# Four of eight router weights spread by DMA and multiplied on GpSimd, and the depthwise taps summed in PSUM, in the last stage of a two-layer MetaFormer kernel

## The chip, the cores and the metric

The kernel runs on one core of one Trainium2 chip. The metric is the device time of one execution in microseconds. A core has five engines that work side by side, each through its own instructions in a fixed order: TensorE (PE in the profile; PEld is its weight load), VectorE (DVE), ScalarE (ACT), GpSimd (POOL) and SyncE (SP), which here issues the DMAs. They wait for each other through semaphores. SBUF and PSUM are the two on-chip memories, both with 128 partitions; products of TensorE land in PSUM, which has eight banks of 128x512 f32.

## The reference

Eight images of 128 channels and 64 x 64 pixels pass through two layers, each a token mixer and a mixture of experts. The change lies in the end of the second layer alone:

```python
    # end of the second mixer (L1_conv)
    out = _ln(out, norm2_w, norm2_b)
    out = out.transpose(0, 2, 1).reshape(B, C, H, W) + seed
    h1 = einsum('bchw,oc->bohw', out, fc1_w) + fc1_b            # 256 hidden channels
    dw = conv_general_dilated(h1, dw_w, (1, 1), 'SAME',
                              feature_group_count=256)           # depthwise, 3 x 3
    h2 = gelu(dw + dw_b)
    ffn = einsum('bohw,co->bchw', h2, fc2_w) + fc2_b
    return out + ffn                                             # added to x outside

    # second mixture of experts (L1_ffn), on layer-normed tokens, 8 experts, top 2
    router_probs = softmax(x @ router_w + router_b)
    top_p, top_i = top_k(router_probs, 2)
    top_p = top_p / sum(top_p)
    expert_out = einsum('bnd,edc->bnec', x, expert_w) + expert_b
    gathered = take_along_axis(expert_out, top_i[..., None], axis=2)
    return einsum('bnk,bnkc->bnc', top_p, gathered)
```

## The kernel before

The layers run one after the other. A selective scan in four directions over eight images takes the first half of the time, then come the first experts, and the second mixer's state-space layers. The last stage, `second_ffn`, is where the change lies. It works on 64 slices: eight images of eight slices, each of 128 channels by 512 pixels, which are eight image rows. All data are f32.

The stage is a software pipeline written as a list of steps. At time t of the loop, the step with offset `at` works on slice t - at, with the late steps first:

```python
            steps = [(0, load), (1, center), (2, scale), (3, hidden), (5, taps), (6, feed), (7, center2), (8, scale2),
                     (9, logits), (9 + RS, weights), (10 + RS, experts)]
```

with RS = 4. A scheduler then gives each engine its fixed order, from dependences, priorities, free buffers and its own costs; a tile pool's `bufs` says how many slices may hold a tile at once. So an instruction may stand some way from where the list has it. The steps are:

- `load`: three DMAs on SyncE's queue (ys, seed and x2; x2 shows as x in the profile).
- `center`, `scale`: layer norm. Two products with a matrix of 1/128 make mean and variance (ln_m, ln_v), VectorE subtracts (xc), ScalarE squares and does the reciprocal root as Ln and Exp (sq), GpSimd multiplies (ys) and adds to seed.
- `hidden`: the two halves of fc1 (h_p in the profile), written by ScalarE with the bias into h1 (h), a padded image of 66 x 66 for each half. Two images are kept.
- `taps`: per half, nine VectorE instructions with a per-partition weight. The first multiplies and adds the bias (L336), eight multiply and add (L339) into dw, an SBUF tile with four buffers. h1 is read at nine shifted places; a slice needs a row of the slices above and below it, which lie in the same padded image.
- `feed`: ScalarE's Gelu in place on dw, two products into f_p, the residual on VectorE and GpSimd (res).
- `center2`, `scale2`: the second layer norm, ending with GpSimd's multiply into yn.
- `logits`: per slice four small products into lg_p; after each fourth slice the router's top 2 for all four, some twenty small VectorE instructions (`route`).
- `weights`: transposes the slice's router weights to 8 rows (pt_p) and ScalarE copies them into pT, a tile of 128 rows that are zero from row 8 on.
- `experts`: a product with expert_b into o_p. Then for each of eight experts: a product of a selection matrix sel8 with pT spreads the expert's weights over 128 partitions (pb_p, L288), VectorE multiplies yn by it (xw, L330), and a product with the expert's matrix adds to o_p. A last VectorE add goes into res, and a DMA stores it (L1636).

Helpers hold the lines that the profile names: L288 is every matmul of `mm`, L330 `tt`, L336 and L339 `ts` and `stt`, L291 `act`. ScalarE swaps its function table around Gelu (two loads per slice). PSUM's eight banks go to the tags n (3 buffers: ln_m, ln_v, h1_p), f (1), lg (1), o (1) and pb (2).

Of the kernel before, what the change touches and what calls it, by code (L numbers as in the profile page):

```python
# [9 lines left out]
F32 = mybir.dt.float32  # L10
# [11 lines left out]
C = 128  # L22
# [256 lines left out]
class Net:  # L279
# [907 lines left out]
    def second_setup(self, pool, ps):  # L1187
# [3 lines left out]
        nc.vector.tensor_copy(self.sel8, bc(self.k("ident")[:, :8], 128))  # L1191
        self.pT = [pool.tile([128, S], F32, name=f"pT{q}") for q in range(2)]
        for t in self.pT:
# [266 lines left out]
    def second_ffn(self):  # L1460


        nc, tc = self.nc, self.tc
        pool = nc.gpsimd
        RS = 4
        NQ = RS * S // 128
# [3 lines left out]
        with tc.tile_pool(name="ff", bufs=1) as pl, tc.tile_pool(name="ffw", bufs=2) as wk, \  # L1470
                tc.tile_pool(name="ffps", bufs=1, space=PSUM) as ps:

            h1 = [[pl.tile([128, 66, 66], F32, name=f"h1_{q}{h}") for h in range(2)] for q in range(2)]
            for t in (*h1[0], *h1[1]):
                nc.vector.memset(t[:, 0:66:65, :], 0.0)
                nc.vector.memset(t[:, 1:65, 0:66:65], 0.0)
            gm = pl.tile([C, self.nb], F32, name="gm")
            nc.vector.tensor_reduce(gm, self.gms, AX.X, ALU.add)
            self.ts(gm, gm, 1.0 / L, ALU.mult)
            p = ps.tile([C, S], F32, tag="n", bufs=3, name="gm_p")  # L1480
            self.mm(p[:, : self.nb], self.mix.rearrange("p q c -> p (q c)"), gm)
# [19 lines left out]
            def squares(v, x):  # L1501

                p = bank("n", 3, "ln_m")
                self.mm(p, self.k("mean"), x)
                v["xc"] = tile_("xc", 4)
                self.tt(v["xc"], x, p, ALU.subtract)
                v["sq"] = tile_("sq", 4)
                self.act(v["sq"], v["xc"], AF.Square)

            def scaled(v, out):  # L1510
                p = bank("n", 3, "ln_v")
                self.mm(p, self.k("mean"), v["sq"])
                self.rsqrt(v["sq"], p, self.k("e5"))
                self.tt(out, v["xc"], v["sq"], ALU.mult, pool)
# [13 lines left out]
            def hidden(n):  # L1528
                v = made[n]
                b, s, sg = place(n)  # L1530
                for h in range(2):
                    p = bank("n", 3, "h1_p")
                    self.mm(p, self.w("fc1_w")[:, h * 128 : (h + 1) * 128], v["seed"])
                    self.act(h1[b % 2][h][:, 1 + 8 * s : 9 + 8 * s, 1:65], p.rearrange("p (r q) -> p r q", q=64),
                             AF.Identity, bias=self.w(f"fc1_b{h}"))

            def taps(n):
                v = made[n]
                b, s, sg = place(n)
                gelus = v["a"] = []  # L1540
                for h in range(2):
                    a = wk.tile([128, 8, 64], F32, name="dw", bufs=4)
                    for k in range(9):
                        x = h1[b % 2][h][:, 8 * s + k // 3 : 8 * s + k // 3 + 8, k % 3 : k % 3 + 64]
                        w = self.w(f"dw_w{h}")[:, k : k + 1]
                        if k == 0:
                            self.ts(a, x, w, ALU.mult, self.w(f"dw_b{h}"), ALU.add)
                        else:
                            self.stt(a, x, w, a, ALU.mult, ALU.add)
                    gelus.append(a)  # L1550

            def feed(n):
                v = made[n]
                self.silus_done([self.act(a, a, AF.Gelu_apprx_tanh) for a in v["a"]])
                f = bank("f", 1, "f_p")
                for h, a in enumerate(v.pop("a")):
                    self.mm(f, self.w(f"fc2_w{h}"), a.rearrange("p r q -> p (r q)"), start=h == 0, stop=h == 1)
                x = v["res"] = tile_("res", RS + 5)
                self.stt(x, f, self.w("fc2_b"), v["seed"], ALU.add, ALU.add)
                self.tt(x, x, v["x2"], ALU.add, pool)  # L1560
# [4 lines left out]
            def scale2(n):  # L1565
                v = made[n]
                v["yn"] = tile_("yn", RS + 4)
                scaled(v, v["yn"])
# [44 lines left out]
            def weights(n):  # L1613
# [3 lines left out]
                for c in range(S // 128):  # L1617
                    nc.tensor.transpose(p[:8, c * 128 : (c + 1) * 128], routed["now"][:, n % RS * (S // 128) + c, :],
                                        self.k("ident"))
                nc.scalar.copy(self.pT[n % 2][:8], p[:8])  # L1620

            def experts(n):
                v = made[n]
                b, s, sg = place(n)
                pT = self.pT[n % 2]
# [88 lines left out]
```

## Time and profile before

| | |
|---|---|
| runs, median (lowest to highest) of 3 | 21109.04 us (21099.6 to 21120.56) |
| profiled execution | 21100.1 us |
| its span | 21098.0 us |
| PE busy | 16896.5 us, 80% |
| DVE busy | 15973.0 us, 76% |
| ACT busy | 11555.9 us, 55% |
| POOL busy | 8894.3 us, 42% |
| `second_ffn`: first load issued, end of the span | 19303.83, 21098.0 us |

Shares are of the whole span, and most of it belongs to other stages; `second_ffn` is the last three and a half of the page's 40 slices of the span. The page's groups are by line, so one line of a helper holds operations from all stages, and tiles tell them apart. In a row of the groups the numbers behind the bar are the idle time of the engine just before these instructions and what ended it. Tile names lose their buffer numbers: h is h1, sel is sel8, m is a PSUM tile of the first scan.

### The profile page before, as it was taken

The numbers are of one execution on the slowest core, as the hardware profiler recorded it, in microseconds if no ns is written. First come the engines' busy times: TensorE is split into PE (matmuls) and PEld (weight loads), VectorE is DVE, ScalarE is ACT, GpSimd is POOL, SyncE is SP. The second block draws the span as 40 slices with busy tenths as digits, with TensorE's granted clock in tenths as the row PEclk, the third lists the DMA queues.
The fourth block names the chain that finished last, engine by engine and source line by source line (L and its number), as shares of the span: only waits on it lengthen the run. The fifth ranks groups of instructions, "written<-read, shape, count | busy, mean of one in ns | idle before, by whom it ended". The sixth has DMA issues, their size and how long they took to land. (4 is left out here: it accounts for less than half of the span.)

```text
span 21098.0 us, 301814 instructions
## 1 busy us (share of the span) xinstructions
PE 16896.5 (80%) x112733; PEld 8742.5 (41%) x112733; DVE 15973.0 (76%) x21079; ACT 11555.9 (55%) x17646; POOL 8894.3 (42%) x6004
## 2 busy tenths in 40 slices
PE   6777777777777777777887888888888888887999
PEld 2222222222222222222645666666666666664343
DVE  7979799797988979798354666666666666667886
ACT  6555555555555555555253555555555555555442
POOL 6757577575767757576011111212111121212221
PEclk9989899999999999899687999999999999998999
DMA  4434344343444434344441000000000000001110
GB/s 113 130 105 130 101 132 129 104 129 105 130 110 123 129 104 130 103 132 118 137 130 37 25 27 26 25 27 25 27 26 25 26 25 27 25 27 36 40 42 24
DMA packets 804471, 1616.93 MB, mean 77 GB/s; under 512 B 179579, under 2 KB 411931, under 8 KB 802267
## 3 DMA queue, kind: packets, MB, share of 16 engines
q1 hardware_dynamic: 803006, 1597.61, 27.6%
q8 instruction: 893, 14.63, 0.3%
q14 instruction: 572, 4.69, 0.1%
HBM read 1373.56 MB, written 223.74 MB: 76 GB/s over the span
## 5 line engine op out<-in xcount | busy, mean ns | idle before, releaser
L288 PE MATMUL dA<-parts,expand 128*128 128x512 bf16 x12288 | 3445.5, 390 | 2448.5 <-ACT dA L291 1770.3
L330 POOL TENSOR_TENSOR bx<-xE,B 128x1024 f32<-128x1024 f32 x2048 | 4823.0, 2358 | 703.7 <-DVE dA L622 461.9
L291 ACT ACTIVATE dA<-dA,negA 128x512 f32<-128x512 f32 x4096 | 2709.4, 661 | 3726.2 <-PE dA L288 3703.4
L622 DVE TENSOR_TENSOR_SCAN dA<-dA,last,bx 128x1024 f32<-128x1024 f32 x1536 | 3612.6, 2352 | 175.7 <-ACT dA L291 158.5
L288 PEld LDWEIGHTS <-expand 128*128 128x128 bf16 x12288 | 1195.4, 98 | 5231.3 <-issue 4517.6
L291 ACT ACTIVATE E_cm<-ss_p 128x1024 f32<-128x1024 f32 x2048 | 1976.9, 1030 | 1544.2 <-PE ss_p L288 1542.7
L339 DVE SCALAR_TENSOR_TENSOR E_cm<-E_cm,gm_cm 128x1024 f32<-128x1024 f32 x2048 | 2423.9, 1224 | 512.6 <-ACT E_cm L291 511.9
L330 DVE TENSOR_TENSOR hc<-dA,C 128x1024 f32<-128x1024 f32 x2048 | 2508.6, 1225 | 166.7 <-DVE dA L622 3.2
L1131 POOL COPY Sd_cm<-S_cm 64x128 f32<-64x128 f32 x1024 | 800.0, 781 | 2887.0 <-DVE S_cm L330 2754.0
L330 POOL TENSOR_TENSOR xD_cm<-tok_cm,D_cm 128x256 f32<-128x256 f32 x512 | 413.1, 807 | 2915.0 <-PE y_p L288 2795.1
L288 PE MATMUL y_p<-E_cm,pad_cm 128*32 128x128 f32 x32768 | 1389.7, 286 | 18.3 <-DVE E_cm L339 10.1
L288 PE MATMUL ss_p<-ssB_cm,ssA_cm 128*128 128x512 bf16 x4096 | 1242.6, 420 | 188.4 <-ACT E_cm L291 166.9
L622 DVE TENSOR_TENSOR_SCAN dA<-dA,bx 128x1024 f32<-128x1024 f32 x512 | 1174.1, 2293 | 185.4 <-POOL bx L330 130.2
L288 PE MATMUL y<-hc,kt 128*32 128x512 f32 x8192 | 1199.8, 653 | 26.0 <-DVE hc L330 26.0
L288 PEld LDWEIGHTS y_p<-E_cm,pad_cm 128*32 128x32 f32 x32768 | 940.5, 113 | 388.5 <-issue 240.6
L288 PE MATMUL bc_p<-stk_cm,W_cm 128*128 128x256 f32 x4096 | 1019.2, 392 | 23.8 <-DMA stk_cm<-xs 20.8
L330 DVE TENSOR_TENSOR gm_cm<-g_p,kt 128x1024 f32<-128x1024 f32 x512 | 624.3, 1219 | 505.8 <-PE g_p L288 501.0
L339 DVE SCALAR_TENSOR_TENSOR dw<-h,w_second,dw 128x512 f32<-128x512 f32 x1024 | 854.4, 860 | 5.1 <-ACT h L291 1.0
L291 ACT ACTIVATE tok_cm<-tok_p 128x384 f32<-128x384 f32 x1024 | 503.0, 491 | 605.6 <-PE tok_p L288 450.5
L288 PEld LDWEIGHTS bc_p<-stk_cm,W_cm 128*128 128x128 f32 x4096 | 739.9, 190 | 194.7 <-issue 76.8
L291 ACT ACTIVATE BC_cm<-bc_p 128x1024 f32<-128x1024 f32 x512 | 525.0, 1026 | 536.8 <-PE bc_p L288 532.4
L288 PE MATMUL tok_p<-W_cm,stk_cm 128*128 128x200 f32 x4096 | 761.4, 339 | 0.0
(387 smaller groups left out, 30190.7 us busy)
## 6 DMA issues: line engine op xcount, KB each, us to landing
xE<-dtx_d SPq DMA_DIRECT2D x2048, 512.0 KB
dtx_d<-dtx SPq DMA_DIRECT2D x256, 256.0 KB
x<-x SPq DMA_DIRECT2D x192, 256.0 KB
ssA_cm<-cs_cm SPq DMA_DIRECT2D x3072, 4.0 KB
stk_cm<-xs SPq DMA_DIRECT2D x368, 128.0 KB
stk_cm<-y SPq DMA_DIRECT2D x368, 128.0 KB
x<-in_x_dram SPq DMA_DIRECT2D x64, 256.0 KB
x<-r SPq DMA_DIRECT2D x64, 256.0 KB
```

The lines of the kernel that those rows point to most:

```text
L288: self.ordered(self.nc.tensor.matmul(out, lhsT=lhsT, rhs=rhs, start=start, stop=stop))
L291: i = self.ordered(self.nc.scalar.activation(out, in_, func, **kw))
L330: self.ordered((eng or self.nc.vector).tensor_tensor(out, a, b, op))
L339: self.ordered(self.nc.vector.scalar_tensor_tensor(out=out, in0=a, scalar=s, in1=b, op0=op0, op1=op1))
L622: self.ordered(nc.vector.tensor_tensor_scan(out=t, data0=t, data1=bx.pop(n), initial=0.0 if ch["j"] == 0 else last[:, q : q + 1], op0=ALU. ...
L1131: nc.gpsimd.tensor_copy(Sd[gr, :, g * hi : (g + 1) * hi], S2[gr])
```

## The change

Two edits go together in `second_ffn`.

The router weights of experts 4 to 7 take another way. `weights` writes their four rows of pT to DRAM by a DMA, and a second DMA reads them back to all 128 partitions (pb, 128x2048). A new step `weighted` multiplies yn by them on GpSimd (xwd, 128x512 each). `experts` spreads by a product and multiplies on VectorE for experts 0 to 3 alone; the two kinds alternate in the sum into o_p.

The taps sum into a PSUM tile dw with two buffers instead of SBUF with four; Gelu reads it and writes an SBUF tile. The banks come from n (3 to 2 buffers) and pb (2 to 1). h1 is kept per slice, ten rows of 66, in a ring of four: ScalarE writes a slice's eight rows and also, in instructions of their own, its first and last row into the neighbouring slices' tiles; GpSimd fills the border rows of an image's first and last slice.

`weights` moves one step later, `weighted` two steps behind it, and `experts` three steps later than it was. pT gets four buffers, res and yn three more.

```diff
-        self.pT = [pool.tile([128, S], F32, name=f"pT{q}") for q in range(2)]
+        self.pT = [pool.tile([128, S], F32, name=f"pT{q}") for q in range(4)]
...
+        NP = 4
...
-            h1 = [[pl.tile([128, 66, 66], F32, name=f"h1_{q}{h}") for h in range(2)] for q in range(2)]
-            for t in (*h1[0], *h1[1]):
-                nc.vector.memset(t[:, 0:66:65, :], 0.0)
-                nc.vector.memset(t[:, 1:65, 0:66:65], 0.0)
+            h1 = [[pl.tile([128, 10, 66], F32, name=f"h1_{q}{h}") for h in range(2)] for q in range(4)]
+            for q in h1:
+                for t in q:
+                    nc.vector.memset(t[:, :, 0:66:65], 0.0)
...
-                p = bank("n", 3, "ln_m")
+                p = bank("n", 2, "ln_m")
...
-                p = bank("n", 3, "ln_v")
+                p = bank("n", 2, "ln_v")
...
-                    p = bank("n", 3, "h1_p")
+                    p = bank("n", 2, "h1_p")
                     self.mm(p, self.w("fc1_w")[:, h * 128 : (h + 1) * 128], v["seed"])
-                    self.act(h1[b % 2][h][:, 1 + 8 * s : 9 + 8 * s, 1:65], p.rearrange("p (r q) -> p r q", q=64),
-                             AF.Identity, bias=self.w(f"fc1_b{h}"))
+                    p = p.rearrange("p (r q) -> p r q", q=64)
+                    own = h1[n % 4][h]
+                    if s == 0:
+                        pool.memset(own[:, :1], 0.0)
+                    if s == NS - 1:
+                        pool.memset(own[:, 9:], 0.0)
+                    for to, of in ((own[:, 1:9], p), *([(h1[(n - 1) % 4][h][:, 9:], p[:, :1])] * (s > 0)),
+                                   *([(h1[(n + 1) % 4][h][:, :1], p[:, 7:])] * (s < NS - 1))):
+                        self.act(to[:, :, 1:65], of, AF.Identity, bias=self.w(f"fc1_b{h}"))
...
-                    a = wk.tile([128, 8, 64], F32, name="dw", bufs=4)
+                    a = ps.tile([128, 8, 64], F32, tag="dw", bufs=2, name="dw")
                     for k in range(9):
-                        x = h1[b % 2][h][:, 8 * s + k // 3 : 8 * s + k // 3 + 8, k % 3 : k % 3 + 64]
+                        x = h1[n % 4][h][:, k // 3 : k // 3 + 8, k % 3 : k % 3 + 64]
...
-                self.silus_done([self.act(a, a, AF.Gelu_apprx_tanh) for a in v["a"]])
+                hs = [tile_("gelu", 4) for _ in v["a"]]
+                self.silus_done([self.act(h, a.rearrange("p r q -> p (r q)"), AF.Gelu_apprx_tanh)
+                                 for h, a in zip(hs, v.pop("a"))])
...
-                x = v["res"] = tile_("res", RS + 5)
+                x = v["res"] = tile_("res", RS + 8)
...
-                v["yn"] = tile_("yn", RS + 4)
+                v["yn"] = tile_("yn", RS + 7)
...
-                nc.scalar.copy(self.pT[n % 2][:8], p[:8])
+                pT = self.pT[n % len(self.pT)]
+                nc.scalar.copy(pT[:8], p[:8])
+                d = self.dp.tile([NP, S], F32, name="p_d", bufs=3)
+                nc.sync.dma_start(d, pT[8 - NP : 8])
+                made[n]["pb"] = wk.tile([128, NP, S], F32, name="pb", bufs=2)
+                nc.sync.dma_start(made[n]["pb"], bc(d, 128, 0))
+
+            def weighted(n):
+                v = made[n]
+                v["xw"] = []
+                for e in range(NP):
+                    xw = tile_("xwd", 2 * NP)
+                    self.tt(xw, v["yn"], v["pb"][:, e], ALU.mult, pool)
+                    v["xw"].append(xw)
...
                 for g in range(8):
-                    pb = bank("pb", 2, "pb_p")
-                    self.mm(pb, self.sel8[:, g, :], pT)
-                    xw = tile_("xw", 3)
-                    self.tt(xw, v["yn"], pb, ALU.mult)
-                    self.mm(o, self.w("expert_w")[:, g * 128 : (g + 1) * 128], xw, start=False, stop=g == 7)
+                    e = g // 2 + g % 2 * NP
+                    if e < 8 - NP:
+                        pb = bank("pb", 1, "pb_p")
+                        self.mm(pb, self.sel8[:, e, :], pT)
+                        xw = tile_("xw", 3)
+                        self.tt(xw, v["yn"], pb, ALU.mult)
+                    else:
+                        xw = v["xw"][e - 8 + NP]
+                    self.mm(o, self.w("expert_w")[:, e * 128 : (e + 1) * 128], xw, start=False, stop=g == 7)
...
             steps = [(0, load), (1, center), (2, scale), (3, hidden), (5, taps), (6, feed), (7, center2), (8, scale2),
-                     (9, logits), (9 + RS, weights), (10 + RS, experts)]
+                     (9, logits), (10 + RS, weights), (12 + RS, weighted), (13 + RS, experts)]
```

More of the change, by code (lines that the diff above doesn't have):

```diff
@@ L1479, in second_ffn @@
             self.ts(gm, gm, 1.0 / L, ALU.mult)
-            p = ps.tile([C, S], F32, tag="n", bufs=3, name="gm_p")
+            p = ps.tile([C, S], F32, tag="n", bufs=2, name="gm_p")
             self.mm(p[:, : self.nb], self.mix.rearrange("p q c -> p (q c)"), gm)
@@ L1553, in feed @@
                 v = made[n]
-                self.silus_done([self.act(a, a, AF.Gelu_apprx_tanh) for a in v["a"]])
+                hs = [tile_("gelu", 4) for _ in v["a"]]
+                self.silus_done([self.act(h, a.rearrange("p r q -> p (r q)"), AF.Gelu_apprx_tanh)
+                                 for h, a in zip(hs, v.pop("a"))])
                 f = bank("f", 1, "f_p")
-                for h, a in enumerate(v.pop("a")):
-                    self.mm(f, self.w(f"fc2_w{h}"), a.rearrange("p r q -> p (r q)"), start=h == 0, stop=h == 1)
-                x = v["res"] = tile_("res", RS + 5)
+                for h, a in enumerate(hs):
+                    self.mm(f, self.w(f"fc2_w{h}"), a, start=h == 0, stop=h == 1)
+                x = v["res"] = tile_("res", RS + 8)
                 self.stt(x, f, self.w("fc2_b"), v["seed"], ALU.add, ALU.add)
@@ L1624, in experts @@
                 b, s, sg = place(n)
-                pT = self.pT[n % 2]
+                pT = self.pT[n % len(self.pT)]
                 o = bank("o", 1, "o_p")
```

## The prediction

> **What bounds the kernel now.** The page's span is 21098.0 us and the profiled run took 21100.1, 9 below the median of the runs (21109.04). Everything is summed against 21100.1 and the 9 is added back. Up to the second FFN both programs hold the same instructions in the same order on every engine (two more small fills aside), so I read only the last 1.8 ms. First, busy time by stage: before the first expert (the loop fills), with everything running, and after the last tap (it drains).
>
> ```profile
> core 0: us, PE busy (x) PEld busy (x) DVE busy (x) ACT busy (x) POOL busy (x), PEclk, DMA share, GB/s
> 19285.00:19490.00 205.00, 128.98 (x331) 52.52 (x321) 155.30 (x220) 103.60 (x145) 68.53 (x38) 0.72 0.18 55
> 19490.00:20920.00 1430.00, 1323.51 (x3379) 569.11 (x3378) 1245.29 (x1938) 584.48 (x828) 350.01 (x218) 0.98 0.12 38
> 20920.00:21098.00 178.00, 164.29 (x395) 64.45 (x393) 66.24 (x110) 12.11 (x19) 5.03 (x4) 0.96 0.04 15
> ```
>
> Together 1813 us. TensorE is 93% and VectorE 87% busy in the middle; GpSimd 24%. The timeline of SyncE's queue gives the pace: the ys load before a pair of stores recurs every fourth slice.
>
> ```profile
> 20208.20 0.32 SPq L1499 DMA_DIRECT2D ys<-ys  x1
> ...
> 20310.54 0.32 SPq L1499 DMA_DIRECT2D ys<-ys  x1
> ```
>
> 102.34 us for four slices: 25.6 each. Next, the groups by line, 19600 to 20800 (46.9 slices), and the same operations elsewhere in the trace by tile or line (minimum/median/maximum ns).
>
> ```profile
> L339 DVE SCALAR_TENSOR_TENSOR dw<-h,w_second,dw 128x512 f32<-128x512 f32 x736 | 611.6, 851 | 3.8
> L330 DVE TENSOR_TENSOR xw<-yn,pb_p 128x512 f32<-128x512 f32 x365 | 242.3, 678 | 40.7 <-PE pb_p L288 40.0
> L330 POOL TENSOR_TENSOR ys<-xc,sq 128x512 f32<-128x512 f32 x47 | 85.5, 1819 | 93.7 <-issue 84.4 <-ACT sq L291 9.3
> L336 DVE TENSOR_SCALAR dw<-h,w_second 128x512 f32<-128x512 f32 x92 | 64.9, 707 | 45.3 <-PE f_p L288 45.3
> ```
>
> ```profile
> L339 DVE SCALAR_TENSOR_TENSOR dw<-h,w_second,dw x1024: 730/742/1799, 19322.9 to 20919.4; 128x512 f32<-128x512 f32 x171
> L339 DVE SCALAR_TENSOR_TENSOR m<-sp_u,m x256: 683/696/697, 111.3 to 9882.4; 128x512 f32<-128x512 f32 x128
> ```
>
> ```profile
> L330 DVE TENSOR_TENSOR hc<-dA,C x430: 1223/1225/1226, 4001.1 to 5996.5; 128x1024 f32<-128x1024 f32 x144
> ```
>
> The tap sum dw reads two SBUF tensors: usually 742 ns, but up to 1799, mean 851, and the long ones stand beside GpSimd multiplies, themselves stretched to a mean of 1819. In the scan stage GpSimd is 78% busy (4150 to 4250), yet m<-sp_u,m (one operand and the result in PSUM, the form that dw gets) never passes 697 and hc, with one PSUM operand, never 1226. So GpSimd and VectorE disturb each other where VectorE reads two SBUF tensors, and not where one of them is in PSUM.
>
> By start-to-start times in the timeline, a tap costs VectorE 0.66 us, a first tap 0.46, xw or xc 0.60, res 0.66 and 0.60, the router's small ones 1.6 per slice. Per slice: 16 x 0.66 + 2 x 0.46 + 8 x 0.60 + 2 x 0.60 + 1.26 + 1.6 = 20.3; the stretch adds 16 x 0.109 + 2 x 0.165 = 2.1 (851 and 707 against 742 and 542): 22.4. TensorE issues a 128x512 f32 matmul every 0.43 us, two per product: 50 x 0.43 + 1.3 (logits, transposes) = 22.8. Neither alone makes 25.6; they wait for each other for about 2.8.
>
> **Part by part.** *Four experts lose their spreading matmul and VectorE multiply.* TensorE: 8 x 0.43 = 3.4 less, 19.4 per slice. VectorE: 4 x 0.60 = 2.4 less.
>
> *Tap sums in PSUM.* The stretch goes: 2.1 less. The row m<-sp_u,m has the price, 696; dw also takes a per-partition scalar, so I keep 742 and 0.66. A VectorE instruction that follows directly on one whose PSUM result it reads starts later than one that doesn't: m to dt 0.73, dt to the scan 0.60.
>
> ```profile
> 3008.86 0.69 DVE L330 TENSOR_TENSOR m<-sp_u,m 128x512 f32<-128x512 f32 x1
> 3009.59 0.69 DVE L330 TENSOR_TENSOR dt<-sp_r,m 128x512 f32<-128x512 f32 x1
> 3010.19 2.35 DVE L622 TENSOR_TENSOR_SCAN dA<-dA,last,bx 128x1024 f32<-128x1024 f32 x1
> ```
>
> In the changed order (as the changed program's instructions stand on each engine) the two halves' chains alternate with other work: 10 of 1152 tap instructions follow directly on their own chain, so nothing here; at 0.13 for each of 18 it would be 2.3. The first tap lies between 0.46 and 0.60 (a multiply of the xw form): I add 0.1 in all. VectorE: 20.3 - 2.4 + 0.1 = 18.0.
>
> [...]
>
> *Two PSUM buffers for dw instead of four in SBUF.* The first tap of slice n+1 now waits on ScalarE's Gelu of n for the same half (before: on f_p, 45.3 us in 46.9 slices). After the last tap VectorE still has xc and the other half's first tap to do (0.60 + 0.46); Gelu needs about 0.69 (PSUM source, as sq<-ln_v) when ScalarE stands ready: hidden, or 0.5. If ScalarE is late by a table load (1.28), sq (0.62) and an h write (0.69), some 2.6.
>
> *One pb bank and two n banks instead of two and three.* In the changed order each pb product is followed by one or two other products before the two o products: 0.86 to 1.72 against 0.25 + 0.69 for the multiply. Covered mostly; 0 to 1 us.
>
> *GpSimd's four multiplies.* 4 x 1.27 (undisturbed 128x512, as yt<-yt,zs) = 5.1 to 4 x 1.8 = 7.3; with its own four, 10 to 14 us of a slice. They stand ahead of ys, seed, res and yn on GpSimd, and TensorE's h product waits for seed already (36.0 us, 13 times); but those four lose their stretch (means 1.39 to 1.82 now), so I take 0 net, up to 1.3.
>
> *Spread by DMA.* SyncE gets two issues per slice. The write waits for ScalarE's copy, the spread for the write (2.3 us, as dtx_d issue to xE issue) and for GpSimd's release two slices back; queued behind are stores and the loads of ys, seed and x2, which the order places three or more slices ahead of use. The stages leave two slices of cover; without it a round trip is 2.3 + 4.0 (the longest wait of bx for xE) = 6.3. 1 MB more per slice against a DMA share of 0.12: no collision.
>
> *Edge rows.* 3.5 ScalarE writes of 128x64 per slice at 0.22 (wd<-dec_p): 0.8 on an engine at 41% (584 of 1430). The border fills (32 small ones on GpSimd) and the further buffers of pT, res and yn: nothing that a slice would show.
>
> **The sum.** TensorE 19.4 and VectorE 18.0 bound the slice; waits stay about as before (2.8, less for fewer hand-overs, more for the bank waits): 22.0. The changed order holds 11.8 slices of taps before the first expert (before 9.0), 52.2 in the middle, 11.5 of experts behind the last tap (9.5). Fill: 168/9 = 18.7 per slice; there the stretch is larger (taps 923 ns mean: 16 x 0.18 + 2 x 0.19 = 3.3), some bank waits come back: 16.0. Drain: slices with experts alone follow at 16.8 (21077.58 to 21094.40); now four pairs at about 3.6 and the rest: 15.2, and 18 us of other work as before. Lead-in 37 + 11.8 x 16.0 + 52.2 x 22.0 + 11.5 x 15.2 + 18 = 1567, against 1813: 246 less. 21100.1 - 246 = 20854; with the 9, **20863**.
>
> **Rivals.**
> 1. *Hand-overs shrink too:* TensorE at 19.4 + 1.0. 52.2 x 1.6 = 84 less: 20780. For it: four xw hand-overs fewer of eight (TensorE's idle on xw was 31.8 us). Against: single banks. 0.15.
> 2. *The round trip isn't covered:* routing comes once in four slices, the third and fourth spread of a group wait for GpSimd, and GpSimd then blocks in order. 16 groups x 2 trips x 6.3 = 202 back: 21065, a gain of 44. For: SyncE is one queue. Against: two stages of cover. 0.09.
> 3. *The stretch doesn't go* (the move to PSUM doesn't do what it is for): GpSimd works twice as long, so 2.1 becomes about 4.2, VectorE 22.2 and the slice 25. Fill 18.7: 246 - 157 - 32 = 57 gained, 21052. Against: the 697 and 1226 maxima. 0.05.
> 4. *Slower: Gelu in the tap loop.* First taps wait for Gelu, which stands in ScalarE's order behind sq and an h write that waits for TensorE, which waits for seed from a busier GpSimd. It decides from a VectorE stall of 8.7 per slice (18.0 + 8.7 = 26.7, where 52.2 x 4.7 eats the 246). Table load, Gelu, sq, h write, edge: 1.28 + 0.69 + 0.62 + 0.69 + 0.22 = 3.5; with the longest waits for seed (3.0) and a ys load (4.2) 10.7: a slice of 28.7, 350 more, 21213. For it: one loop over four engines. Against: that all come late in every slice. 0.07.
>
> **Numbers.** The forecast has 0.64: its slice from 21 to 24, that is 20811 to 20967. With rival 1 and part of 2, the range 20765 to 21000 holds 8 in 10. About 0.2% (42 us) is what a measurement of this kernel can tell from no change. Rivals 2 and 3 lie near that border, so: faster 0.87, same 0.05, slower 0.08.
>
> **What would show it.** Right: dw (then into PSUM) with a mean near 742 and a maximum below 800; GpSimd's multiplies near 1.27 with ten microseconds or more per slice; four slices in about 88 us; TensorE still over 85% busy. Wrong: first taps idle on Gelu by more than 3 us a slice (4), GpSimd idle on the spread's DMA (2), taps still stretched (3), or single-bank waits of xw that hold TensorE near 25.

## The result, and the profile after

The changed kernel took 20883.06 us, the median of four runs (20869.88 to 20900.35), against 21114.8 us for the kernel before in the same measurement: a ratio of 0.9892, with a 95% interval of 0.9877 to 0.9906, or 232 us less. The forecast was 20863. The profiled span is 20879.7 us.

The windows of the changed kernel's profile, at its own fill, middle and drain, and a last row for 1000 us in the middle:

```profile
core 0: us, PE busy (x) PEld busy (x) DVE busy (x) ACT busy (x) POOL busy (x), PEclk, DMA share, GB/s
19285.00:19520.00 235.00, 154.68 (x491) 64.78 (x487) 166.40 (x269) 133.01 (x214) 60.67 (x55) 0.76 0.18 56
19520.00:20740.00 1220.00, 1117.80 (x2956) 501.89 (x2956) 1063.91 (x1705) 617.36 (x999) 558.53 (x465) 0.96 0.27 93
20740.00:20880.00 140.00, 115.71 (x264) 43.57 (x263) 32.34 (x47) 3.44 (x6) 38.56 (x30) 1.00 0.21 69
19600.00:20600.00 1000.00, 923.04 (x2438) 415.07 (x2438) 881.66 (x1401) 522.57 (x852) 453.05 (x376) 0.97 0.27 93
```

TensorE is still 92% and VectorE 88% busy, GpSimd went from 24% to 45%. The pace is now read from the issues of the first pair of spread DMAs of each group of four slices, in the timeline of SyncE's queue:

```profile
20147.97 2.54 SPq L1634 DMA_DIRECT2D p_d<-pT  x2
...
20233.45 2.54 SPq L1634 DMA_DIRECT2D p_d<-pT  x2
...
20323.03 2.54 SPq L1634 DMA_DIRECT2D p_d<-pT  x2
```

85.5 and 89.6 us for four slices, 21.4 and 22.4 each, against 25.6 before. Over 48 slices of the middle, from first tap to first tap, the pace is 22.0 us a slice, and 25.9 in the kernel before. Now the groups of the same 1000 us (45 slices), and the taps by tile over the whole stage:

```profile
L339 DVE SCALAR_TENSOR_TENSOR dw<-h,w_second,dw 128x512 f32<-128x512 f32 x723 | 513.1, 748 | 0.0
L330 POOL TENSOR_TENSOR xwd<-yn,pb 128x512 f32<-128x512 f32 x176 | 226.7, 1303 | 178.7 <-issue 107.5 <-PE o_p L288 42.5 <-DMA pb<-p_d 28.5
L330 DVE TENSOR_TENSOR xw<-yn,pb_p 128x512 f32<-128x512 f32 x181 | 123.9, 685 | 51.8 <-PE pb_p L288 50.3
L336 DVE TENSOR_SCALAR dw<-h,w_second 128x512 f32<-128x512 f32 x92 | 74.5, 810 | 45.9 <-ACT gelu L291 45.7
L330 POOL TENSOR_TENSOR ys<-xc,sq 128x512 f32<-128x512 f32 x45 | 57.8, 1284 | 65.9 <-ACT sq L291 65.9
L330 DVE TENSOR_TENSOR q<-q,kt 128x128 f32<-128x128 f32 x22 | 25.7, 1169 | 0.0
L330 DVE TENSOR_TENSOR q<-q,m 128x128 f32<-128x128 f32 x11 | 13.9, 1267 | 0.0
L330 DVE TENSOR_TENSOR m<-m,m 128x16 f32<-128x16 f32 x11 | 12.7, 1154 | 0.0
```

```profile
L339 DVE SCALAR_TENSOR_TENSOR dw<-h,w_second,dw x1024: 737/749/758, 19342.4 to 20703.9; 128x512 f32<-128x512 f32 x171
```

The taps' mean fell from 851 to 748 and their longest from 1799 to 758; GpSimd's ys fell from 1819 to 1284. The stretch is gone where the prediction looked for it. It came up in another place: the router's small operations read two SBUF tensors too, and in the same 1000 us of the kernel before q<-q,kt took 281 ns, q<-q,m 281 and m<-m,m 163. There another of them was stretched, e<-e,m:

```profile
L330 DVE TENSOR_TENSOR e<-e,m 128x128 f32<-128x128 f32 x10 | 11.6, 1163 | 0.0
L330 DVE TENSOR_TENSOR q<-q,kt 128x128 f32<-128x128 f32 x20 | 5.6, 281 | 0.0
```

All small operations of the router together went from 1.6 to 2.5 us a slice. The mean of 1169 for q<-q,kt holds one operation of 8.78 us (see the last section); without it the mean is 0.8.

In what follows the **stage time** is counted from the first L339 tap (the first start in the row above) to the end of the span, and split at the last tap. In the profiles of this study that first tap starts between 19304.7 and 19344.3, a scatter of the stages ahead, and this leaves it out. Before: 1596.5 with taps and 178.6 behind them, 1775.1 in all. After: 1361.5 and 175.8, 1537.3 in all. That is 237.8 less. The split depends on how many slices still wait for their experts at the last tap: 10 in the kernel before and in "taps in PSUM alone" with two pb banks, 14 with one pb bank, and 12 in all others (counted by the res<-res,o_p additions behind the last tap).

| kernel | median us | ratio to before (95%) | taps | behind | stage against before |
|---|---|---|---|---|---|
| changed | 20883.06 | 0.9892 (0.9877 to 0.9906) | 1361.5 | 175.8 | -237.8 |
| taps in PSUM alone | 21177.1 | 1.0034 (1.0021 to 1.0047) | 1525.8 | 306.7 | +57.4 |
| the same, two pb banks | 21147.41 | 1.0025 (1.0015 to 1.0034) | 1636.9 | 179.6 | +41.4 |
| spread by DMA and GpSimd alone | 21041.93 | 0.9969 (0.9958 to 0.9980) | 1537.5 | 158.3 | -79.3 |
| the same, VectorE multiplies | 21030.53 | 0.9968 (0.9957 to 0.9979) | 1546.4 | 147.6 | -81.1 |
| changed, VectorE multiplies | 20880.25 | 0.9896 (0.9882 to 0.9911) | 1365.5 | 181.8 | -227.8 |
| changed, first tap on ScalarE | 20860.35 | 0.9882 (0.9866 to 0.9899) | 1351.6 | 176.5 | -247.0 |
| both of these | 20845.52 | 0.9874 (0.9859 to 0.9888) | 1330.3 | 182.8 | -262.0 |
| changed, two pb banks | 20860.76 | 0.9891 (0.9875 to 0.9908) | 1379.1 | 151.5 | -244.5 |
| changed, three dw banks | 20821.91 | 0.9873 (0.9858 to 0.9888) | 1324.4 | 175.8 | -274.9 |
| six experts spread | 20846.75 | 0.9878 (0.9861 to 0.9894) | 1362.3 | 143.2 | -269.6 |
| six spread, three dw banks | 20754.44 | 0.9842 (0.9828 to 0.9855) | 1295.3 | 141.3 | -338.5 |
| all eight spread, three dw banks | 20770.81 | 0.9840 (0.9826 to 0.9855) | 1310.1 | 121.9 | -343.1 |

Ratios are against runs of the kernel before on the same chip (medians of 21092 to 21115). The difference of the medians and that of the stage times agree within some 17 us in every row; differences of some 10 us between two rows rest on the stage times of one profile each, and their ratios' intervals overlap.

### The profile page after: what moved, and what is told of

It reads as the page before. It is cut to its first block, busy times and chain, and to the rows that moved or that the text cites. A ratio compares the mean times of both kernels' runs of the same rounds, so it can differ in the third digit from the quotient of the medians.

```text
span 20879.7 us, 301414 instructions
## 1 busy us (share of the span) xinstructions
PE 16692.1 (80%) x112221; PEld 8667.2 (42%) x112221; DVE 15762.0 (75%) x20825; ACT 11598.1 (56%) x17867; POOL 9127.7 (44%) x6292
## 5 line engine op out<-in xcount | busy, mean ns | idle before, releaser
L339 DVE SCALAR_TENSOR_TENSOR E_cm<-E_cm,gm_cm 128x1024 f32<-128x1024 f32 x2048 | 2424.6, 1224 | 514.4 <-ACT E_cm L291 514.4
L288 PE MATMUL bc_p<-stk_cm,W_cm 128*128 128x256 f32 x4096 | 1019.0, 392 | 24.1 <-DMA stk_cm<-xs 20.8
L288 PE MATMUL g_p<-BC_cm 64*128 64x128 f32 x8192 | 746.7, 309 | 0.3
```

Of the source, the lines that this page charges most:

```text
L288: self.ordered(self.nc.tensor.matmul(out, lhsT=lhsT, rhs=rhs, start=start, stop=stop))
L339: self.ordered(self.nc.vector.scalar_tensor_tensor(out=out, in0=a, scalar=s, in1=b, op0=op0, op1=op1))
```

## The experiments

The scheduler makes an order for each kernel anew. So every run below differs from the changed kernel by its edit and by the order that came of it, and a difference of a few tens of microseconds can't be put down to the edit's own work alone.

**Each half of the change alone.** Taps in PSUM, but all experts through TensorE:

```diff
-        NP = 4
+        NP = 0
...
-                nc.sync.dma_start(d, pT[8 - NP : 8])
...
-                nc.sync.dma_start(made[n]["pb"], bc(d, 128, 0))
...
-                    e = g // 2 + g % 2 * NP
+                    e = g
...
-                     (9, logits), (10 + RS, weights), (12 + RS, weighted), (13 + RS, experts)]
+                     (9, logits), (9 + RS, weights), (10 + RS, experts)]
```

> The taps' sums lie in PSUM (two banks, with the tiled h and the spare Gelu tile), but all eight experts are spread by TensorE and multiplied by VectorE, with the one pb bank and two n banks of the changed kernel. Theory (both halves of the change are needed, since TensorE holds the slice as soon as VectorE's stretch is gone): dw falls to a mean of about 749 ns, VectorE's slice to 20.3 us, but TensorE keeps 22.8 and the slice is 24.0 to 24.8: 50 to 100 us below the kernel before, 21010 to 21065. Rival A (the stretch alone carried the gain): 190 to 240 below, 20875 to 20925. Rival B (TensorE alone): no faster than the kernel before. Rival C (two dw banks and one pb bank cost much): slower than the kernel before, with VectorE idle on Gelu or TensorE idle on xw by over 3 us a slice.

It was slower than the kernel before, by 73 us. The taps did what was foreseen (mean 749) and their part of the stage got 71 us shorter, but the part behind them grew by 128. Part of that is a shift: four more slices of experts are left over at the last tap. The other part is their pace. There TensorE and VectorE take turns over the single pb bank, as TensorE's timeline shows:

```profile
21072.24 1.13 PE L288 MATMUL o_p<-xw,w_second 128*128 128x512 f32 x2 [0.78 <-DVE xw L330]
21073.21 1.02 PE L288 MATMUL pb_p<-pT,sel 128*128 128x512 f32 x2
21075.01 1.13 PE L288 MATMUL o_p<-xw,w_second 128*128 128x512 f32 x2 [0.78 <-DVE xw L330]
21075.97 1.02 PE L288 MATMUL pb_p<-pT,sel 128*128 128x512 f32 x2
```

2.77 us for each expert (21072.24 to 21075.01), 22.1 a slice (the last eleven res additions start from 20951.6 to 21172.9), where it was 16.8. Four slices more at 22.1 are 88 us, and ten at 5.3 more each are 53. The same with two pb banks tests that reading:

```diff
-                f = bank("f", 1, "f_p")
+                f = bank("n", 2, "f_p")
...
-                        pb = bank("pb", 1, "pb_p")
+                        pb = bank("pb", 2, "pb_p")
```

> The kernel with the taps' sums in PSUM alone (all eight experts through TensorE and VectorE), but with two pb banks; f_p takes a bank of the group n. With one pb bank it took 25.0 us a slice in the middle and 21.7 for each slice of the drain (the kernel before 25.6 and 16.8), and was 73 us slower. Theory (the single bank's chain of product, multiply and product is what that kernel lost; without it TensorE's 22.8 and some waits set the slice): drain back to 17 a slice, middle 24 to 25: 20 to 100 us below the kernel before, 21005 to 21085. Rival A (the stretch alone carried the gain of the change): 20875 to 20925. Rival D (it isn't the single pb bank): as the kernel with one, 21150 or more.

Half of the theory held: behind the taps ten slices are left again, at 16.8 each, and that part is back at 179.6. The other half fell. The part with taps grew to 1636.9, more than before the change, and the time, 21147, lies next to the 21150 of rival D. The window of the middle here and in the kernel before (first row), and two rows of 5 us behind a TensorE gap of 3.6 us, which the timeline puts down to yn:

```profile
19600.00:20600.00 1000.00, 930.21 (x2395) 399.96 (x2394) 865.56 (x1352) 418.88 (x598) 247.14 (x156) 0.99 0.13 41
...
19600.00:20600.00 1000.00, 911.45 (x2269) 400.30 (x2267) 779.16 (x1277) 423.07 (x688) 189.89 (x164) 0.94 0.12 39
...
20160.00:20165.00 5.00, 3.69 (x14) 2.84 (x15) 2.05 (x5) 2.71 (x5) 0.87 (x1) 0.50 0.19 56
20165.00:20170.00 5.00, 5.00 (x13) 2.14 (x12) 3.64 (x6) 3.49 (x7) 0.00 (x0) 0.87 0.00 0
```

VectorE is only 78% busy, TensorE 91% at a granted clock of 0.94 (0.99 in the same window of the kernel before). 72 first taps make 36 slices, 27.8 us each: 22.8 / 0.94 = 24.3 of work (an estimate that scales the prediction's count with the clock), 2.5 of idle time (89 of 1000) and 1.0 that I can't place. Of the 89 us idle, 48.5 stand before the logits' product, on yn. So without TensorE's relief the freed VectorE wins nothing: it waits 221 of the 1000 us. That TensorE then holds the slice is read from these shares. That the two banks which dw takes from its products (pb or n) cost it more than before is an argument; which of the four users of n makes the gaps wasn't tried.

The other half: the spread by DMA and GpSimd, with dw in SBUF, four buffers, Gelu in place, and the banks of before.

```diff
-                    a = ps.tile([128, 8, 64], F32, tag="dw", bufs=2, name="dw")
+                    a = wk.tile([128, 8, 64], F32, name="dw", bufs=4)
```

> Four experts are spread by DMA and multiplied by GpSimd as in the changed kernel, but the taps' sums stay in SBUF (four buffers, Gelu in place) and the pb and n banks are two and three as before. Theory: GpSimd, busy about twice as long, stretches the taps on both sides: dw mean from 851 to 900 to 960 ns, GpSimd's 128x512 operations from 1.27 to 1.7 to 1.9 us; VectorE's slice stays near 22, the slice 24 to 25.5: 0 to 100 us below the kernel before, 21010 to 21110. Rival B (TensorE alone carried the gain): 190 to 240 below, 20875 to 20925. Rival D (GpSimd, stretched to eight times 1.8 and more, comes late with the tables for the h product): slower than the kernel before.

79 us less in the stage, as the theory had it; rival B is out. The groups of the middle:

```profile
L339 DVE SCALAR_TENSOR_TENSOR dw<-h,w_second,dw 128x512 f32<-128x512 f32 x650 | 611.1, 975 | 4.3 <-DVE dw L339 0.5
L330 POOL TENSOR_TENSOR xwd<-yn,pb 128x512 f32<-128x512 f32 x161 | 239.2, 1504 | 135.4 <-PE o_p L288 87.1 <-DMA pb<-p_d 42.9 <-issue 5.1
```

The taps stretch to a mean of 975 (900 to 960 was expected), GpSimd's operations less than expected (1504 here, 1700 to 1900 expected), and the chain of waits lies on the taps for 42.1% of the middle; VectorE is busy for 958 of 1000 us, and is the bound. To see whether that is GpSimd's new load, VectorE took the multiplies:

```diff
-                    self.tt(xw, v["yn"], v["pb"][:, e], ALU.mult, pool)
+                    self.tt(xw, v["yn"], v["pb"][:, e], ALU.mult)
```

> Four experts' weights come by DMA, as in the changed kernel, but VectorE multiplies by them (GpSimd has its own four operations alone), and the taps' sums stay in SBUF, with the banks of the kernel before. TensorE has 19.4 us a slice, VectorE what it had before, 22.4, and 0.3 to 0.8 more (the four multiplies read two SBUF tensors now and can be stretched too). Theory (TensorE's relief is worth little as long as VectorE carries the stretch): dw mean near 851, the slice 23.5 to 25: 30 to 120 below the kernel before, 20985 to 21075. Rival B (TensorE alone carried the gain): 20875 to 20925, with dw still near 850. Rival D (without TensorE's products between them the stretched operations fall together and VectorE holds 25.6): within 25 of the kernel before.

The time is within the theory's range and the same as with GpSimd (-81.1 and -79.3), but not for its reason: the taps' mean is 946, not near 851, although GpSimd has only its four operations of before (busy for 249 us of 1000, 247 in the kernel before). So how long the taps stretch does not follow GpSimd's load alone; that what falls together in time counts as well is an argument, which no run tests.

Alone, then, the halves bring +57 (or +41) and -79; together -238. Each takes the load off one of two engines that by the prediction's sums were both near 22.6 us a slice, and the other stays. For the spread alone the trace shows it (VectorE 96% busy); for the taps alone the banks cost something too, and the two aren't parted.

**The multiplies on GpSimd.** The same edit of the multiply in the changed kernel:

> The changed kernel with the four multiplies by the spread weights on VectorE instead of GpSimd; the weights still come by DMA, TensorE's work is that of the changed kernel. VectorE gains 4 x 0.66 = 2.6 us a slice, less what the router's small operations were stretched by (up to 3), GpSimd goes back to 24%. Theory: VectorE's 87% of 22.2 us is 19.3, with 2.6 more and about 1 to 2 of stretch less 20 to 21; the slice 22.2 to 23.7: 0 to 100 us above the changed kernel, 20885 to 20985, the router's q<-q,kt back at about 281 ns. Rival E (VectorE is the bound in full): 2.6 x 64 = 166 above, 21050. Rival G (GpSimd's multiplies are late and hold the o products): below the changed kernel.

Just below the theory's range: the ratio is 0.9896 to 0.9892, the stage 10 us longer. VectorE goes from 882 to 939 busy in 1000 and waits less; q<-q,kt is at 423, not back at 281, though GpSimd has only the four operations that it had in the kernel before; which of the router's operations is hit changes with the order (here q<-i,kt most, at 588; with the first tap on ScalarE pw<-pw,q, at 997). For the time it hardly matters who multiplies; what the spread by DMA saves is TensorE's product.

**The first tap.** L336 into PSUM takes 811 ns (542 in SBUF before). ScalarE instead:

```diff
-                            self.ts(a, x, w, ALU.mult, self.w(f"dw_b{h}"), ALU.add)
+                            self.act(a, x, AF.Identity, scale=w, bias=self.w(f"dw_b{h}"))
```

> The changed kernel with the first tap of each half on ScalarE (one activation with scale and bias into the PSUM bank) in place of VectorE's 811 ns operation. VectorE loses 2 x 0.72 = 1.4 us a slice, ScalarE (46% busy) gains 2 x 0.7. Theory (TensorE's 19.4 to 20.3 and the hand-overs set the slice, VectorE has a few per cent to spare): 10 to 50 us below the changed kernel, 20835 to 20875. Rival E (VectorE is the bound): 1.4 x 64 = 90 below, 20795. Rival F (the loop through ScalarE's order holds the taps: Gelu, then the next first tap on the same engine): slower than the changed kernel, with the second tap idle on ScalarE.

The median is 23 us lower and the stage 9 shorter, at the small end of what the theory foresaw, and the intervals of the two ratios overlap. VectorE now waits more for TensorE (87.1 us before xw and 56.6 before xc in the middle, where it was 50.3 and 2.8). GpSimd's group in the middle shows another wait that comes forward when VectorE has time:

```profile
L330 POOL TENSOR_TENSOR xwd<-yn,pb 128x512 f32<-128x512 f32 x179 | 229.7, 1298 | 252.9 <-DMA pb<-p_d 115.6 <-issue 104.5 <-PE o_p L288 30.4
```

115.6 us of waiting for the spread weights instead of 28.5. So the multiplies went to VectorE as well:

> The changed kernel with the first tap on ScalarE and the four multiplies by the spread weights on VectorE. With the first tap on ScalarE alone GpSimd waited 2.5 us a slice for the spread weights, in order ahead of its other work, and that DMA stood in the chain of waits; here GpSimd has its own four operations only. Theory (TensorE's 20.3 and the small waits set the slice, whoever multiplies): VectorE at 78% gets 2.6 us more, about 90%; 20830 to 20880, no more than 30 from the kernel with the first tap alone (20860). Rival A (GpSimd's wait for the DMA ate the first tap's gain): 50 to 70 below that, 20790 to 20810. Rival B (VectorE is the bound): above the changed kernel, 20900 or more.

15 us better than the first tap alone in stage and median, with ratios whose intervals overlap: the theory's range, and only a small part of what rival A asked.

**The banks.** In the changed kernel f_p can move to the group n, which frees a bank for pb or for dw (the edit of f_p as above, and `bufs=3` for dw in the second).

> The changed kernel with two pb banks again: f_p takes a bank of the group n (two banks, now for ln_m, ln_v, h_p and f_p) and leaves its own to pb. Theory (TensorE's 20.3 us of work per slice and about 1.9 of many small waits make the 22.2; in the changed order the single pb bank is mostly covered): xw's waits for pb_p fall from 50 us in 1000 to below 25, the time by 0 to 30 us against the changed kernel: 20855 to 20885. Rival A (the single bank holds the slice): 50 to 75 below, 20810 to 20835. Rival B (the group n is what is short): slower than the changed kernel, with ln or h products idle for a bank.

> The changed kernel with three dw banks: f_p takes a bank of the group n, and its own goes to dw. Theory (the first taps' wait for Gelu is small): that wait falls from 46 us in 1000 to below 10, the time by 0 to 30 us against the changed kernel: 20855 to 20885. Rival C (the hand-over of two dw banks from Gelu holds the slice): 45 to 65 below, 20820 to 20840. Rival B (the group n is what is short): slower than the changed kernel.

A second pb bank brings 7 us in the stage; xw's wait for pb_p didn't fall (61.9 us against 50.3, where below 25 was expected), and the part behind the taps got 24 shorter while the part with them got 18 longer. In both runs f_p is a fourth user of n's two banks, and xc's wait for ln_m grew from 2.8 us to 25.8 and 23.5: some of what the freed bank gives may be taken back there, and neither run parts the two. A third dw bank brings 37, and here rival C's range was met, not the theory's: the price of Gelu's hand-over. The first taps' group, with three dw banks:

```profile
L336 DVE TENSOR_SCALAR dw<-h,w_second 128x512 f32<-128x512 f32 x95 | 75.8, 808 | 5.1 <-ACT gelu L291 5.1
```

45.7 us of first taps waiting for Gelu in 45 slices are 1.0 a slice; with 5.1 left the slice is 21.3 (47 in 1000). What made that wait in the changed kernel can be seen in its timelines, ScalarE's, TensorE's and VectorE's:

```profile
20123.10 0.60 ACT L291 ACTIVATE gelu<-dw 128x512 f32<-128x512 f32 x1
20123.59 0.62 ACT L291 ACTIVATE sq<-xc 128x512 f32<-128x512 f32 x1
20125.77 0.69 ACT L291 ACTIVATE h<-h_p,w_second 128x512 f32<-128x512 f32 x1 [1.56 <-PE h_p L288]
20126.36 0.59 ACT L291 ACTIVATE gelu<-dw 128x512 f32<-128x512 f32 x1
...
20123.75 1.13 PE L288 MATMUL f_p<-gelu,w_second 128*128 128x512 f32 x2 [1.88 <-ACT gelu L291]
20124.71 1.02 PE L288 MATMUL h_p<-seed,w_second 128*128 128x512 f32 x2
...
20126.98 0.81 DVE L336 TENSOR_SCALAR dw<-h,w_second 128x512 f32<-128x512 f32 x1 [2.44 <-ACT gelu L291]
```

The second half's Gelu stands in ScalarE's order behind an h write; the h product stands in TensorE's order behind f_p, which waits for the first half's Gelu. That is the loop of the prediction's rival 4 at a small size, with f_p in the place of seed: 34.7 of the 45.7 us are first taps behind an h write that waited so. In the kernel with three dw banks no h write stands between the two Gelus of any slice of the middle (in the changed kernel one does in all 45), so its gain belongs to the bank and to that order together.

**TensorE's work.** If TensorE held the slice at 22.2, taking two more experts off it should show.

```diff
-        NP = 4
+        NP = 6
...
-                x = v["res"] = tile_("res", RS + 8)
+                x = v["res"] = tile_("res", RS + 7)
...
-                    xw = tile_("xwd", 2 * NP)
+                    xw = tile_("xwd", 6)
...
-                    e = g // 2 + g % 2 * NP
+                    e = [0, 2, 3, 4, 1, 5, 6, 7][g]
```

> The changed kernel with six of the eight experts spread by DMA and multiplied by GpSimd (six xwd tiles instead of eight, one res tile less, to fit); two experts keep TensorE's product. TensorE loses 2 x 0.86 = 1.7 us a slice (17.7), VectorE 1.2 to 1.3, GpSimd has ten operations of 1.28 (12.8). Theory (TensorE and the hand-overs set the slice of 22.2): 20.5 to 21.5, that is 45 to 110 below the changed kernel, 20775 to 20840. Rival A (Gelu's hand-over of the two dw banks holds the slice as it stands): within 30 of the changed kernel, with more idle on Gelu. Rival B (GpSimd, in order behind the spread's DMA, becomes the bound): slower than the changed kernel, with seed and yn late.

The gain of 32 us lies behind the taps alone (143.2 against 175.8). The part with taps stayed at 1362.3, within a microsecond. The first taps' group and the window of the middle:

```profile
L336 DVE TENSOR_SCALAR dw<-h,w_second 128x512 f32<-128x512 f32 x90 | 73.0, 811 | 91.5 <-ACT gelu L291 91.5
```

```profile
19600.00:20600.00 1000.00, 869.95 (x2251) 402.96 (x2250) 783.22 (x1305) 508.89 (x848) 563.11 (x466) 0.92 0.34 117
```

The first taps wait twice as long for Gelu, TensorE idles more, and its granted clock falls to 0.92: rival A, but for the gain behind the taps. Two other things changed: nearly all of that wait (86.7 us) is now for the first half's Gelu, and VectorE waits 31.8 us in 1000 for a free res tile, of which there is one less here. With three dw banks the same step was tried again:

> Six experts spread by DMA and multiplied by GpSimd, as in the kernel that kept its slice at 22.2 us though TensorE had 1.7 us less to do (20847, its first taps idle on Gelu for 91.5 us in 1000), but with three dw banks; f_p takes a bank of the group n. Theory (the hand-over of two dw banks from Gelu held that slice, not TensorE's work): the wait falls below 15 us in 1000, the slice to 20.5 to 21.3, and the time by 58 to 110 to 20735 to 20790. Rival A (every relief is taken up by the other hand-overs of the loop and by TensorE's lower granted clock in its gaps): the wait goes, but the slice stays above 21.7, the time within 30 of 20847. Rival B (GpSimd, with ten operations in order behind the spread's DMA, sets the slice): as A, with GpSimd over 60% busy and its wait for pb grown over 55 us in 1000.

The theory's ranges for time and slice were met: 20754, 48 slices in 1000 us (20.8 each). The wait for Gelu is 20.8 us, where it said below 15. Rival B's signs are there (GpSimd 60% busy, 72.1 us of waiting for pb), but not the slice above 21.7 that it foresaw; the wait for a res tile is still 21.7 us, so it wasn't that which held the slice. With a third dw bank two more experts bring 29 us with taps and 34.5 behind them. So it was the hand-over of the two dw banks, in the order that went with them, that held the slice with six experts, and a part of the changed kernel's.

Last, all eight by DMA (two tiles of four), three multiplied on GpSimd and five on VectorE, the first tap on ScalarE, the pb bank given to dw. The core of the edit:

```diff
-                    if e < 8 - NP:
-                        pb = bank("pb", 1, "pb_p")
-                        self.mm(pb, self.sel8[:, e, :], pT)
+                    if e >= 3:
                         xw = tile_("xw", 3)
-                        self.tt(xw, v["yn"], pb, ALU.mult)
+                        self.tt(xw, v["yn"], v["pb"][e // 4][:, e % 4], ALU.mult)
```

> All eight experts' weights come by DMA (in two tiles of four, three buffers), so that TensorE makes no spreading product and the pb bank goes to dw as a third; three experts are multiplied on GpSimd, five on VectorE, the first tap is on ScalarE. TensorE: 22.8 - 16 x 0.43 = 15.9 us a slice; VectorE: 16 x 0.66 + 5 x 0.66 + 1.2 + 1.3 + 1.6 to 4 for the router's = 18 to 20.4; GpSimd seven of 1.28; 2 MB a slice by DMA. Theory (with TensorE relieved VectorE sets the slice): 19 to 21, with the drain at some 10 a slice: 100 to 250 below the changed kernel, 20635 to 20785. Rival A (the loop of hand-overs from engine to engine holds the slice near 22, not one engine's work): 0 to 70 below. Rival B (two DMA spreads a slice, through SyncE's one queue, come late): slower than the changed kernel, with xw or xwd idle on the DMA of pb.

The group of xw in the middle:

```profile
L330 DVE TENSOR_TENSOR xw<-yn,pb 128x512 f32<-128x512 f32 x237 | 201.8, 867 | 89.4 <-PE o_p L288 89.0
```

112 us below the changed kernel, at the slow end of the range; the slice of 21.1 is just above the 19 to 21 that the theory gave. xw reads two SBUF tensors here and stretches from 685 to a mean of 867. In its middle no engine is over 90% busy (TensorE 870 of 1000 at a clock of 0.90, VectorE 891), which points to the hand-overs as what sets the slice; several things were changed at once here, and no run tests that. This and the kernel with six experts and three dw banks are the fastest of the study, and not to be told apart.

## Why the prediction was right, and what was mis-sized

*The stretch goes (2.1 a slice).* Right: taps at 749 with a maximum of 758, GpSimd's multiplies at 1293, as the rows of m<-sp_u,m and hc had said. But it wasn't the whole: the router's small operations, which the sum left at their 1.6 us, now take more of it. The three groups shown come to 52.3 us in 45 slices, 1.2 each; at the former means they would be 11.1, or 0.25. And the rule that two SBUF tensors are needed is too narrow for the kernel before: its first tap, with one SBUF tensor and per-partition scalars, was stretched as well (531 to 1501 ns, in the prediction's own sum 2 x 0.165).

*The first tap (0.1 a slice in all).* Mis-sized. Its duration went from 542 to 811, and its start to the next one's from 0.46 to about 0.72 (two in a row last 1.53 in the timeline of the kernel with the taps alone, less 0.81): 0.5 a slice, outside the bounds of 0.46 and 0.60. The nearest rows had the result in SBUF.

*VectorE 18.0.* Measured 882 / 45 = 19.6: the two items above are 0.4 and 0.9 of the 1.6 missing.

*TensorE 19.4 and waits of 2.8.* TensorE's busy time is 923 / 45 = 20.5, its idle time 1.7; the granted clock went from 0.99 to 0.97 (19.4 / 0.97 = 20.0, an estimate). One term was 1.1 short and the other 1.1 long, so the slice of 22.0 (22.2 measured) is better than its parts. It is not all luck: the 2.8 was what a sum of 22.8 left of 25.6, and in the kernel before TensorE's busy time is 930 / 38.5 = 24.2 a slice and its idle time 1.8. So the same work of 1.1 to 1.4 us was missing from the product count in both kernels and was carried over among the waits, and the true idle time stayed as it was, as the prediction took the waits to do.

*The Gelu wait (0 to 0.5).* Mis-sized: 1.0 a slice, and the run that took it away gained 37 us, 0.6 a slice. The cover that was named (xc and the other half's first tap) is there, but ScalarE doesn't stand ready: for most of this wait the h write in its order holds it, as rival 4 described. The stall of 8.7 of rival 4 was never near.

*One pb bank (0 to 1).* Not contradicted in the changed order: a second bank brought 7 us in all, net of f_p's move into n. The cover is the order: in the kernel without it, the same bank cost 5.3 us for each slice behind the taps.

*GpSimd's multiplies, 0 net.* Right within some 10 us; the kernel with VectorE's multiplies shows it from the other side.

*The DMA spread is covered.* Right for the slice: GpSimd waits 28.5 us in 45 slices for pb, 0.6 each. Rival 2's mechanism appears when VectorE is relieved (115.6 us, 2.6 each).

*A later tap in PSUM (742 ns and 0.66 kept).* Right: dw with PSUM in and out took 749 ns where dw in SBUF took 742 undisturbed, 7 more. In the kernel before, xw with a PSUM operand and tn<-tn,tsq without one lay as close, at medians of 678 and 684.

*The sum.* Predicted 246 for the stage, measured 238. Fill (first tap to first pb product at 19546.0) 204 us or 17.3 for each of the 11.8 slices, where 16.0 was taken; middle 22.2, where 22.0 was; drain 176, where 11.5 x 15.2 + 18 = 193 was.

*The theory behind it.* "TensorE 19.4 and VectorE 18.0 bound the slice" is right in that neither half alone brought the gain. As far as TensorE, the larger of the two, was to set the slice with its waits, it is wrong: with 1.7 us less TensorE work the slice stayed, and fell only when a third dw bank came with it. Of the gain that the relieved engines offer, the loop through two dw banks keeps a part (the third bank brought 37 us, together with its order), and the clock (0.97, where it was 0.99) another by the author's reading, which no run tests.

## What to carry to other kernels

Where two engines are both near the slice, price a change by what the other one leaves: here one half alone lost 0.3%, the other won 0.3%, and both together won 1.1%. A PSUM bank given to a new use is taken from a hand-over (with one pb bank and all experts on TensorE, a slice behind the taps took 22.1 us where it took 16.8 with two), so ask for each bank group which two engines then take turns. When a stretch is removed from one operation by moving its operand, look for the next one that reads two SBUF tensors (here q<-q,m, which went from 281 to 1267 ns).

## What the hardware showed that was not expected

**A small VectorE operation took 8.8 us beside a run of GpSimd's.** q<-q,kt takes 281 ns when undisturbed. The timeline of VectorE, and that of GpSimd over the same time:

```profile
20334.51 8.78 DVE L330 TENSOR_TENSOR q<-q,kt 128x128 f32<-128x128 f32 x1
...
20345.04 0.68 DVE L330 TENSOR_TENSOR res<-res,o_p 128x512 f32<-128x512 f32 x1
```

```profile
20330.69 5.11 POOL L330 TENSOR_TENSOR xwd<-yn,pb 128x512 f32<-128x512 f32 x4 [2.87 <-DMA pb<-p_d]
20335.71 1.31 POOL L330 TENSOR_TENSOR ys<-xc,sq 128x512 f32<-128x512 f32 x1
20336.93 3.77 POOL L330 TENSOR_TENSOR xwd<-yn,pb 128x512 f32<-128x512 f32 x3
20340.60 1.31 POOL L330 TENSOR_TENSOR seed<-seed,ys 128x512 f32<-128x512 f32 x1
20341.82 1.31 POOL L330 TENSOR_TENSOR xwd<-yn,pb 128x512 f32<-128x512 f32 x1
```

GpSimd ran ten operations without a pause, and VectorE's operation ended (20343.3) within 0.2 us of the last of them. It happened once in this trace, where the next longest of the router's small operations took 1.44 us; in VectorE's timelines of five other kernels (the one before, VectorE's multiplies, the first tap on ScalarE, three dw banks, six spread with three dw banks) none took more than 1.43. What made the difference stays open. That VectorE waited for the whole run of GpSimd's is read from this one coincidence of two ends.

**The gap then cost TensorE twice.** TensorE waited 8.18 us for that res:

```profile
20345.77 2.08 PE L288 MATMUL o_p<-pT,w_second 128*128 128x512 f32 x2 [8.18 <-DVE res L330]
```

```profile
20340.00:20345.00 5.00, 0.00 (x0) 0.00 (x0) 5.00 (x6) 0.00 (x0) 3.13 (x3) 0.68 0.00 0
20345.00:20350.00 5.00, 4.23 (x8) 1.75 (x9) 5.00 (x11) 0.57 (x1) 0.00 (x0) 0.50 0.14 54
20350.00:20355.00 5.00, 5.00 (x13) 3.04 (x12) 2.17 (x5) 3.72 (x5) 1.27 (x1) 0.50 0.73 253
```

Its clock (third figure from the end) had been 1.00 from 20335 to 20340. It stood at 0.50 for more than nine microseconds after the gap, while TensorE worked, and was 0.96 from 20355 to 20360. The two matmuls of a product took 2.08 us at 0.50 (20345.77) and 1.02 at 1.00 (20360.44). By the author's reading this is one reason why relief of TensorE paid less than its microseconds; no run parts it from the others. TensorE was idle for 77 us of 1000 in the changed kernel, 130 with six experts spread (82 with three dw banks) and 130 with eight, and the mean clock of the middle went from 0.97 to 0.92 with six experts spread (0.94 with three dw banks) and 0.90 with eight.
